# Layers of local attention: output product turned round, probabilities divided before they are transposed, scores and outputs in one group each, and a new order of the parts

## The chip, the cores and the metric

The kernel runs on one NeuronCore of a Trainium2 chip. The metric is the device time of one launch in microseconds. The names of the engines are those of the profile: PE is TensorE (PEld its weight loads), DVE is VectorE, ACT is ScalarE, POOL is GpSimd, SP issues the DMAs.

## What is computed

The reference is a network of eight residual stages on x of 2048 rows by 128 features, all in fp32. Two of the eight are the same stage, `L1_ffn`, with the same weights; the rest (three attention stages, a mixture of experts twice, an attention with a linear kernel) is not touched. Cut to what matters, `L1_ffn` is six times:

```python
# attention with a window: 16 heads of 64, blocks of 32 tokens that look at their own and the block before
qkv = shift_tokens(x) @ Wqkv                       # 128 -> 3 x 1024
q, k = l2norm(q) * q_scale, l2norm(k) * k_scale    # per head of 64
q, k = rotary(q) * scale, rotary(k) / scale
sim = einsum('bhwie,bhwje->bhwij', q, look(k)) * 8 # 32 x 64 per block
attn = softmax(where(mask, -max, sim), -1)
out = einsum('bhwij,bhwje->bhwie', attn, look(v))
x = out @ Wo + x
# feed-forward
xn = layernorm(shift_tokens(x)) * g + b
a, gate = split(xn @ W1 + b1)                      # 2 x 341
x = a * gelu(gate) @ W2 + b2 + x
```

## The kernel before

x is kept transposed (features in partitions, tokens along the free dimension). Each `L1_ffn` is one `Layers` object. It works on tiles of 128 tokens: 6 layers x 2 sequences x 8 tiles = 96 tiles, numbered m. Two `Layers` runs make 192 tiles.

The work of a tile is cut into parts, each a method that issues a few instructions on one engine. `turns` is a software pipeline: turn n goes through the words of `ORDER` once, and a word `name:late` issues that part for tile m = n - late. The feed-forward parts (`BY_BLOCK`) work on four tiles at once and run when m is a multiple of 4, so each of four successive turns holds other feed-forward parts. Inside `manual_schedule` PE, ACT, DVE and POOL execute their instructions in exactly the order in which `turns` issues them; there is no other scheduler. SP's DMAs are not in that list of engines.

```python
for n in range(min(lates), last + max(lates)):
    for stage, args, late, step in order:
        m = n - late
        if 0 <= m < last and m % step == 0:
            stage(m, *args)
```

The parts of one tile in the order of the data, with their lines in the kernel before. The digits after a name in `ORDER` are its arguments: s (0 for q, 1 for k), then u or c, j or r (a half).

- `project` s,u (L1448, PE): one 128x512 half of q or k, into a PSUM bank of the pool `pj` (four banks, shared with v, the outputs, y and the feed-forward).
- `squares` s,u (L1457, ACT) reads that bank into `sq`; `rotate` s,u (L1477, DVE, two instructions) reads the same bank and multiplies it by the rotary tables into `t1` and `t2` (two buffers each).
- `halves` s (L1483, POOL) adds the two halves of `sq`; `lengths` s (L1489, DVE) sums them per head; `inverses` (L1502 to L1504, ACT) makes 1/length.
- `join` s (L1494, POOL) adds `t1` and `t2` into `raw` and so frees the t buffers; `scale` s (L1509, POOL) multiplies by 1/length.
- `flip` s,c (L201 `tqk`, PE): four transposes into a bank of tag `tp` (two banks); `heads` s,c (L1527, ACT) copies them to qT or kT. `carry` (L1542, POOL) hands the last 32 keys to the next tile.
- `project_v` r (L1550, PE), `values` r (L1559, ACT), `windows` r (SP DMAs, `vw_l<-v_l`): v, rearranged so that each block's 64 keys lie in 64 partitions.
- `scores` part 0 and 1 (L1588 the mask in bf16, L1597, PE): products with 64 rows and 32 columns of the array, two banks of tag `big`.
- `below_max` j (L1606, L1607, DVE), `exps` j (L1611, ACT, in place in `pr`, two buffers), `sums` (L1619, L1621, DVE): softmax without the division.
- `flip_p` j (L201 `tpr`, PE) transposes the undivided probabilities, `probabilities` j (L1635, ACT) copies them to `pT`.
- `outputs` part 0 and 1 (L1647, PE): for each block and head a product with `pT` (64 x 32) as the stationary operand and `vw` (64 x 64) as the moving one; tokens come out in partitions, features along the free dimension. Two `pj` banks.
- `divide` r (L1655, DVE) multiplies a bank of outputs by 1/sum into `on`; `flip_o` r (L201 `to`, PE) transposes it back, four transposes each; `features` r (L1672, ACT) copies it to `outT`.
- `project_out` (L1679, PE) makes y, `add_out` (L1693, DVE) adds it to x.
- Feed-forward: `ffn_flip`, `ffn_stats`, `ffn_dev`, `ffn_norm`, `ffn_back`, `ffn_gain` (norm), `gate_in` c and `gate` c (L1753, L1763; Gelu, with a load of the ACT table before it and one back at the end), `value_in` c and `value` c (L1774, L1782), `ffn_out` (L1789), `ffn_add` (L1695).

Of the kernel before, what the change touches and what calls it, by code (L numbers as in the profile page):

```python
# [18 lines left out]
P = 128  # L19
# [11 lines left out]
DEPTH, LH, LD, LW = 6, 16, 64, 32  # L31
# [54 lines left out]
class Net:  # L86
# [288 lines left out]
    def attn_a1(self, key):  # L375
        nc, tc = self.nc, self.tc
        scale = 1.0 / DH**0.5
        with ExitStack() as ctx:
# [166 lines left out]
            def fin(k):  # L545
# [23 lines left out]
    def attn_b1(self, key):  # L569
# [5 lines left out]
        with ExitStack() as ctx:  # L575
# [165 lines left out]
            def xt(k):  # L741
# [309 lines left out]
class Experts:  # L1051
# [223 lines left out]


ORDER = """
    value_in1:11 halves0:-2 join0:-2 add_out:3 flip11:0 divide0:2 divide1:2 project_v0:0 ffn_flip:7
    heads01:0 flip_p0:1 gate_in0:9 heads11:0 value_in0:11 lengths1:-1 value1:11 value_in2:10 values0:0
    scores0:0 lengths0:-2 inverses:-1 project10:-2 ffn_back:8 flip_p1:1 ffn_stats:7 gate0:9 value0:11  # L1280
    ffn_out:11 ffn_dev:7 squares10:-2 sums:1 ffn_norm:7 project11:-2 carry:0 project00:-3 value2:10
    rotate10:-2 scores1:0 probabilities0:1 squares11:-2 project_v1:0 ffn_gain:8 probabilities1:1
    flip_o0:2 scale1:-1 ffn_add:11 gate_in2:9 flip_o1:2 windows0:0 rotate11:-2 squares00:-3 values1:0
    scale0:-1 gate_in1:9 rotate00:-3 features0:2 features1:2 below_max0:0 halves1:-2 gate2:9
    below_max1:0 project01:-3 flip10:-1 gate1:9 squares01:-3 exps0:0 outputs0:1 join1:-2 heads10:-1
    rotate01:-3 project_out:2 flip00:-1 heads00:-1 exps1:0 outputs1:1 flip01:-1 windows1:0
"""
BY_BLOCK = (
    "ffn_flip", "ffn_stats", "ffn_dev", "ffn_norm", "ffn_back", "ffn_gain", "gate_in", "gate",
# [4 lines left out]
class Layers:  # L1294
# [281 lines left out]

    def scores(self, m, part):
        nc, st = self.nc, self.get(m)  # L1580
        key = self.name(m)
        if part == 0:
            st["sc"] = [self.ps.tile([P, 8, 64], F32, tag="big", name=f"sc_{key}_{j}") for j in range(2)]
            first = self.place(m)[2] == 0
            for c in range(4):
                for j in range(2):
                    rows = slice(64 * j, 64 * j + 64)
                    nc.tensor.matmul(  # L1588
                        st["sc"][j][ts(c, 32)].rearrange("p h k -> p (h k)"), self.identb[rows, :],
                        self.wide[rows, 1 if first and c == 0 else 0, :], start=True, stop=False,  # L1590
                    )
        sc = st["sc"]
        for hp in range(4 * part, 4 * part + 4):
            for c in range(4):
                for j in range(2):
                    rows = slice(64 * j, 64 * j + 64)
                    nc.tensor.matmul(  # L1597
                        sc[j][ts(c, 32), hp, :], st["q"][rows, hp, ts(c, 32)],
                        st["k"][rows, hp, ds(32 * c, 64)], start=False, stop=(hp == 7),
                    )  # L1600
# [14 lines left out]
    def sums(self, m):  # L1615
        nc, st, key = self.nc, self.get(m), self.name(m)
        sm = self.small.tile([P, 2, 8], F32, tag="sm", name=f"sm_{key}")
        for j in range(2):
            nc.vector.tensor_reduce(sm[:, j], st["p", j], AX.X, ALU.add)  # L1619
        inv = st["inv"] = self.small.tile([P, 2, 4, 2], F32, tag="inv", name=f"inv_{key}")  # L1620
        nc.vector.reciprocal(inv, sm.rearrange("p j (q r) -> p r q j", r=2))  # L1621

# [11 lines left out]
        pt = st["pT", j] = self.sp.tile([P, 4, P], F32, tag="pT", name=f"pT_{self.name(m)}_{j}", bufs=4)  # L1634
        self.nc.scalar.copy(pt, st["tpr", j])  # L1635

    def outputs(self, m, part):
        nc, st, key = self.nc, self.get(m), self.name(m)
        if part == 0:
            st["av"] = [self.pj.tile([P, 4, 2, LD], F32, tag="pj", name=f"av_{key}_{r}") for r in range(2)]  # L1640
        av = st["av"]
        for q in range(2 * part, 2 * part + 2):
            for j in range(2):
                for c in range(4):
                    for r in range(2):
                        rows = slice(64 * r, 64 * r + 64)
                        nc.tensor.matmul(  # L1647
                            av[r][ts(c, 32), q, j, :], st["pT", j][rows, q, ts(c, 32)],
                            st["vw"][rows, c, ts(2 * q + j, LD)], start=True, stop=True,
                        )  # L1650

    def divide(self, m, r):
        st = self.get(m)
        on = st["on", r] = self.sp.tile([P, 4, 2, LD], F32, tag="on", name=f"on_{self.name(m)}_{r}")
        self.nc.vector.tensor_tensor(  # L1655
            on, st["av"][r], st["inv"][:, r, :, :, None].to_broadcast([P, 4, 2, LD]), ALU.mult
        )

    def flip_o(self, m, r):
        st = self.get(m)
        st["to", r] = self.net.to_psum(
            self.ps, "tp", lambda q: st["on", r][:, q].rearrange("p j d -> p (j d)"),
            f"to_{self.name(m)}_{r}",
        )

    def features(self, m, r):
        st = self.get(m)
        if r == 0:  # L1670
            st["o"] = self.qp.tile([P, 8, P], F32, tag="outT", name=f"outT_{self.name(m)}")
        self.nc.scalar.copy(st["o"].rearrange("p (q r) t -> p r q t", r=2)[:, r], st["to", r])  # L1672

    def project_out(self, m):
        i, b, a = self.place(m)
# [293 lines left out]
```

## Time and profile before

| | |
|---|---|
| time, median of 3 runs | 3995.49 us (3991.46 to 3996.87) |
| span of the profiled execution | 3987.0 us (its total is not given on the page) |
| first and last `y_l` group (L1679) | starts at 637.1 and 3957.2 us |
| busy PE / DVE / ACT / POOL | 96% / 78% / 61% / 64% of the span |
| mean granted clock of PE | 0.970 of full speed |
| busy in 606 to 2217 and 2387 to 3987 us, inside the two Layers runs (3211 us) | PE 3182.8, DVE 2555.2, ACT 2073.7, POOL 2173.4 us |
| DMA over the span | 281 MB, mean 71 GB/s |

How to read it. A line of a group gives the source line, the engine, the operation, out<-in by tile names, the shapes, the count; then after the bar the busy time, the mean duration of one in ns; then the idle time of that engine just before these instructions and what ended it. Busy PE is modelled from pipelined matmuls: neighbouring groups overlap in the list, so the cost of a group is best taken from its start to the start of the next one. One fp32 matmul is two records. In the chain of waits each piece is what the end of the run was waiting for at that time.

### The profile page before, as it was taken

The page shows a single profiled execution, that of the slowest core. Times are in us where ns is not written, and L with a number is a line of the kernel's source. Part 1 is how long each engine was busy: PE and PEld are TensorE (multiplying, and loading weights), DVE is VectorE, ACT ScalarE, POOL GpSimd, SP SyncE. Part 2 cuts the span into 40 slices and gives each one's busy share as a digit, 9 for nine tenths or more (in the row PEclk, how much of TensorE's full clock was granted, in tenths as well). Part 3 has the DMA queues.
Part 4 walks back from the last instruction along what each step waited for, and adds up shares of the span by engine and source line. Part 5 has one row for each costly group of instructions (what it writes and reads, how often), then busy time and mean ns, then how long its engine had stood idle before and what let it go on. Part 6 is the DMA issues. An engine that isn't in the chain of part 4 may idle for free.

```text
span 3987.0 us, 156275 instructions
## 1 busy us (share of the span) xinstructions
PE 3825.6 (96%) x67372; PEld 2521.5 (63%) x67372; DVE 3116.1 (78%) x6012; ACT 2414.0 (61%) x4582; POOL 2535.5 (64%) x1638
## 2 busy tenths in 40 slices
PE   7898979999999999999999779999999999999998
PEld 5646436666666666666666446666666666666665
DVE  7775877778787878787887667887878787878786
ACT  3444437766666666666666458666666666666665
POOL 4541448776766667767675467766767767666662
PEclk8899979999999999999999779999999999999999
DMA  3030313232333333323222033333333323332222
GB/s 87 2 85 8 79 62 75 67 92 69 78 84 75 78 78 73 88 72 77 63 70 67 9 95 70 75 85 75 86 71 73 92 68 77 85 76 67 66 68 54
DMA packets 217397, 281.11 MB, mean 71 GB/s; under 512 B 52493, under 2 KB 108682, under 8 KB 216586
## 3 DMA queue, kind: packets, MB, share of 16 engines
q1 hardware_dynamic: 216714, 271.12, 27.9%
q8 instruction: 536, 8.78, 1.0%
q14 instruction: 147, 1.20, 0.1%
HBM read 69.46 MB, written 3.28 MB: 18 GB/s over the span
## 4 chain that ended last, share of the span: by engine, by line
PE 87%; DVE 6%; DMA 2%; POOL 2%; ACT 1%; issue 1%; SPq 0%; DVEq 0%; POOLq 0%; ACTq 0%
PE pj_l L1448 17%; PE y_l L1679 9%; PE pv_l L1550 9%; PE tqk_l L201 9%; PE av_l L1647 8%; PE sc_l L1597 7%; PE tpr_l L201 4%; PE to_l L201 4%; PE fg_l L1753 3%; PE fy_l L1789 3%; PE fa_l L1774 3%; PE sc_l L1588 2%; DMA f0share_e<-f0d_e 1%; PE f0S_e L1239 1%; DVE t_l L1477 1%
## 5 line engine op out<-in xcount | busy, mean ns | idle before, releaser
L1477 DVE TENSOR_TENSOR t_l<-pj_l,rot_l 128x512 f32<-128x512 f32 x1536 | 968.1, 684 | 368.6 <-ACT sq_l L1457 356.6
L1494 POOL TENSOR_TENSOR raw_l<-t_l,t_l 128x1024 f32<-128x1024 f32 x384 | 907.8, 2364 | 532.5 <-DVE on_l L1655 285.0
L1448 PE MATMUL pj_l<-wqkv_l,x_l 128*128 128x512 f32 x1536 | 785.9, 614 | 6.5 <-DVE t_l L1477 4.2
L1509 POOL TENSOR_TENSOR raw_l<-raw_l,rn_l 128x1024 f32<-128x1024 f32 x384 | 723.2, 1902 | 94.6 <-ACT rn_l L1504 87.4
L1483 POOL TENSOR_TENSOR sq_l<-sq_l 128x512 f32<-128x512 f32 x384 | 490.8, 1278 | 311.8 <-ACT sq_l L1457 308.7
L1457 ACT ACTIVATE sq_l<-pj_l 128x512 f32<-128x512 f32 x768 | 461.5, 603 | 369.6 <-PE pj_l L1448 367.6
L201 PE MATMUL tqk_l<-ident_sb,raw_l 128*128 128x128 f32 x3072 | 452.7, 278 | 15.5 <-POOL raw_l L1509 13.9
L1527 ACT COPY qT_l<-tqk_l 128x512 f32<-128x512 f32 x384 | 224.8, 585 | 387.9 <-PE tqk_l L201 387.8
L201 PEld LDWEIGHTS tqk_l<-ident_sb,raw_l 128*128 128x128 f32 x3072 | 356.4, 142 | 160.7 <-issue 121.3
L1550 PE MATMUL pv_l<-wqkv_l,x_l 128*128 128x512 f32 x768 | 416.4, 624 | 6.1 <-DVE ln_xn_fl L1733 5.3
L1679 PE MATMUL y_l<-outT_l,wo_l 128*128 128x128 f32 x3072 | 393.7, 281 | 0.0
L1597 PEld LDWEIGHTS sc_l<-kT_l,qT_l 64*32 64x32 f32 x24576 | 295.4, 105 | 155.5 <-issue 145.1
L1679 PEld LDWEIGHTS y_l<-outT_l,wo_l 128*128 128x128 f32 x3072 | 357.5, 191 | 18.3 <-issue 1.0
L1448 PEld LDWEIGHTS pj_l<-wqkv_l,x_l 128*128 128x128 f32 x1536 | 256.3, 192 | 172.1 <-issue 111.2
L1647 PE MATMUL av_l<-vw_l,pT_l 64*32 64x64 f32 x24576 | 360.5, 224 | 2.1 <-issue 1.7
L1559 ACT COPY v_l<-pv_l 128x512 f32<-128x512 f32 x384 | 225.1, 586 | 225.4 <-PE pv_l L1550 205.5
L1655 DVE TENSOR_TENSOR on_l<-av_l,inv_l 128x512 f32<-128x512 f32 x384 | 247.4, 686 | 121.5 <-PE av_l L1647 121.3
L1647 PEld LDWEIGHTS av_l<-vw_l,pT_l 64*32 64x32 f32 x24576 | 294.2, 105 | 70.0 <-issue 63.6
L1597 PE MATMUL sc_l<-kT_l,qT_l 64*32 64x64 f32 x24576 | 329.8, 223 | 0.3 <-issue 0.3
L201 PEld LDWEIGHTS tpr_l<-ident_sb,pr_l 128*128 128x128 f32 x1536 | 189.1, 141 | 152.3 <-issue 116.8
L1607 DVE TENSOR_TENSOR pr_l<-sc_l,mx_l 128x512 f32<-128x512 f32 x384 | 265.6, 692 | 13.2
L201 PEld LDWEIGHTS to_l<-ident_sb,on_l 128*128 128x128 f32 x1536 | 183.2, 141 | 128.4 <-issue 110.9
(317 smaller groups left out, 6208.9 us busy)
## 6 DMA issues: line engine op xcount, KB each, us to landing
vw_l<-v_l SPq DMA_DIRECT2D x3024, 64.0 KB
wqkv_l<-in_Wqkv SPq DMA_DIRECT2D x36, 512.0 KB
f0share_e<-f0d_e SPq DMA_DIRECT2D x64, 256.0 KB
rot_l<-in_rotary SPq DMA_DIRECT2D x24, 512.0 KB
wo_l<-in_Wo SPq DMA_DIRECT2D x12, 512.0 KB
w_l<-in_W SPq DMA_DIRECT2D x12, 341.0 KB
a0rows<-a0both SPq DMA_DIRECT2D x4, 512.0 KB
a0qk<-a0rows SPq DMA_DIRECT2D x32, 64.0 KB
```

Of the source, the lines that this page charges most:

```text
L201: self.nc.tensor.transpose(tp[:, c, :], src(c), self.ident)
L1448: self.nc.tensor.matmul(pj.rearrange("p h d -> p (h d)"), self.x[b][0][:, ts(a, P)], self.w[i]["qkv"][:, ds(INNER * s + 512 * u, 512)], st ...
L1457: self.nc.scalar.activation(st["sq", s][:, u], st["pj", s, u], AF.Square)
L1477: self.nc.vector.tensor_tensor(to, st["pj", s, u], tabs[:, k, None, ts(w, LD // 2)].to_broadcast(half), ALU.mult)
L1483: self.nc.gpsimd.tensor_tensor(sq[:, 0], sq[:, 0], sq[:, 1], ALU.add)
L1494: self.nc.gpsimd.tensor_tensor(r.rearrange("p h u d -> p u h d"), st["t1", s], st["t2", s], ALU.add)
L1509: self.nc.gpsimd.tensor_tensor(r, r, st["rn"][:, ts(s, LH), None].to_broadcast([P, LH, LD]), ALU.mult)
L1550: self.nc.tensor.matmul(pj, self.x[b][0][:, ts(a, P)], self.w[i]["qkv"][:, ds(2 * INNER + 512 * r, 512)], start=True, stop=True,)
L1597: nc.tensor.matmul(sc[j][ts(c, 32), hp, :], st["q"][rows, hp, ts(c, 32)], st["k"][rows, hp, ds(32 * c, 64)], start=False, stop=(hp == 7),)
L1607: nc.vector.tensor_tensor(p, st["sc"][j], mx[:, :, None].to_broadcast([P, 8, 64]), ALU.subtract)
L1647: nc.tensor.matmul(av[r][ts(c, 32), q, j, :], st["pT", j][rows, q, ts(c, 32)], st["vw"][rows, c, ts(2 * q + j, LD)], start=True, stop=True,)
L1679: self.nc.tensor.matmul(y[:, 0:P], self.w[i]["o"][:, c, :], st["o"][:, c, :], start=(c == 0), stop=(c == 7))
```

## The change

Scores and outputs are issued in one group each instead of two parts. The outputs are formed by features: `vw` (64 x 64) is now the stationary operand and `pT` (64 x 32) the moving one, so features come out in partitions and `features` copies the banks straight to `outT`. `flip_o` goes, and the tile `on` with it. The division moves from the outputs to the probabilities: `divide` j multiplies `pr` by 1/sum in place after `sums` and before `flip_p`. `ORDER` is written anew, with the earliest part at -4 instead of -3, outputs at 2 instead of 1, and other positions for nearly all parts.

```diff
 ORDER = """
-    value_in1:11 halves0:-2 join0:-2 add_out:3 flip11:0 divide0:2 divide1:2 project_v0:0 ffn_flip:7
-    heads01:0 flip_p0:1 gate_in0:9 heads11:0 value_in0:11 lengths1:-1 value1:11 value_in2:10 values0:0
-    scores0:0 lengths0:-2 inverses:-1 project10:-2 ffn_back:8 flip_p1:1 ffn_stats:7 gate0:9 value0:11
-    ffn_out:11 ffn_dev:7 squares10:-2 sums:1 ffn_norm:7 project11:-2 carry:0 project00:-3 value2:10
-    rotate10:-2 scores1:0 probabilities0:1 squares11:-2 project_v1:0 ffn_gain:8 probabilities1:1
-    flip_o0:2 scale1:-1 ffn_add:11 gate_in2:9 flip_o1:2 windows0:0 rotate11:-2 squares00:-3 values1:0
-    scale0:-1 gate_in1:9 rotate00:-3 features0:2 features1:2 below_max0:0 halves1:-2 gate2:9
-    below_max1:0 project01:-3 flip10:-1 gate1:9 squares01:-3 exps0:0 outputs0:1 join1:-2 heads10:-1
-    rotate01:-3 project_out:2 flip00:-1 heads00:-1 exps1:0 outputs1:1 flip01:-1 windows1:0
+    add_out:3 gate2:10 values0:0 exps1:0 exps0:0 scale1:-1 lengths1:-2 flip00:-1 flip01:-1 outputs:2
+    heads00:-1 heads01:-1 sums:0 value_in2:11 flip10:-1 values1:0 halves0:-3 project10:-3
+    features0:2 flip11:-1 value_in0:10 lengths0:-3 features1:2 divide0:0 ffn_back:8 heads10:-1
+    value2:11 join1:-2 project11:-3 rotate10:-3 heads11:-1 divide1:0 project00:-4 squares10:-3
+    squares11:-3 halves1:-3 value0:10 gate_in0:9 inverses:-2 ffn_gain:8 ffn_flip:7 gate_in1:9
+    value_in1:10 scores:-1 ffn_out:11 rotate11:-3 ffn_stats:7 join0:-3 rotate00:-4 scale0:-2
+    ffn_dev:7 project01:-4 gate0:9 windows0:0 squares00:-4 gate1:9 flip_p0:0 flip_p1:0 squares01:-4
+    gate_in2:9 ffn_norm:7 probabilities0:0 value1:10 ffn_add:11 probabilities1:0 project_v0:-1
+    rotate01:-4 carry:-1 below_max0:-1 project_out:2 windows1:0 below_max1:-1 project_v1:-1
 """
...
-    def scores(self, m, part):
+    def scores(self, m):
...
-        for hp in range(4 * part, 4 * part + 4):
+        for hp in range(8):
...
-        inv = st["inv"] = self.small.tile([P, 2, 4, 2], F32, tag="inv", name=f"inv_{key}")
-        nc.vector.reciprocal(inv, sm.rearrange("p j (q r) -> p r q j", r=2))
+        inv = st["inv"] = self.small.tile([P, 2, 8], F32, tag="inv", name=f"inv_{key}")
+        nc.vector.reciprocal(inv, sm)
+
+    def divide(self, m, j):
+        p = self.get(m)["p", j]
+        self.nc.vector.tensor_tensor(
+            p, p, self.get(m)["inv"][:, j, :, None].to_broadcast([P, 8, 64]), ALU.mult
+        )
...
-    def outputs(self, m, part):
+    def outputs(self, m):
...
-            st["av"] = [self.pj.tile([P, 4, 2, LD], F32, tag="pj", name=f"av_{key}_{r}") for r in range(2)]
-        for q in range(2 * part, 2 * part + 2):
-            for j in range(2):
-                for c in range(4):
+        av = st["av"] = [self.pj.tile([P, 4, P], F32, tag="pj", name=f"av_{key}_{r}") for r in range(2)]
+        for q in range(4):
+            for c in range(4):
+                for j in range(2):
                     for r in range(2):
                         rows = slice(64 * r, 64 * r + 64)
                         nc.tensor.matmul(
-                            av[r][ts(c, 32), q, j, :], st["pT", j][rows, q, ts(c, 32)],
-                            st["vw"][rows, c, ts(2 * q + j, LD)], start=True, stop=True,
+                            av[r][ts(j, LD), q, ts(c, 32)], st["vw"][rows, c, ts(2 * q + j, LD)],
+                            st["pT", j][rows, q, ts(c, 32)], start=True, stop=True,
                         )
-    def divide(self, m, r):
-        st = self.get(m)
-        on = st["on", r] = self.sp.tile([P, 4, 2, LD], F32, tag="on", name=f"on_{self.name(m)}_{r}")
-        self.nc.vector.tensor_tensor(
-            on, st["av"][r], st["inv"][:, r, :, :, None].to_broadcast([P, 4, 2, LD]), ALU.mult
-        )
-    def flip_o(self, m, r):
...
-        self.nc.scalar.copy(st["o"].rearrange("p (q r) t -> p r q t", r=2)[:, r], st["to", r])
+        self.nc.scalar.copy(st["o"].rearrange("p (q r) t -> p r q t", r=2)[:, r], st["av"][r])
```

More of the change, by code (lines that the diff above doesn't have):

```diff
@@ L1574, in windows @@
                 nc.sync.dma_start(to, self.get(m - 1)["v"][96:128, r, :])
-    def scores(self, m, part):
+    def scores(self, m):
         nc, st = self.nc, self.get(m)
         key = self.name(m)
-        if part == 0:
-            st["sc"] = [self.ps.tile([P, 8, 64], F32, tag="big", name=f"sc_{key}_{j}") for j in range(2)]
-            first = self.place(m)[2] == 0
-            for c in range(4):
-                for j in range(2):
[L1587 to L1590, printed above, removed]
-                    )
-        sc = st["sc"]
-        for hp in range(4 * part, 4 * part + 4):
+        sc = st["sc"] = [self.ps.tile([P, 8, 64], F32, tag="big", name=f"sc_{key}_{j}") for j in range(2)]
+        first = self.place(m)[2] == 0
+        for c in range(4):
+            for j in range(2):
+                rows = slice(64 * j, 64 * j + 64)
+                nc.tensor.matmul(
+                    sc[j][ts(c, 32)].rearrange("p h k -> p (h k)"), self.identb[rows, :],
+                    self.wide[rows, 1 if first and c == 0 else 0, :], start=True, stop=False,
+                )
+        for hp in range(8):
             for c in range(4):
@@ L1619, in sums @@
             nc.vector.tensor_reduce(sm[:, j], st["p", j], AX.X, ALU.add)
-        inv = st["inv"] = self.small.tile([P, 2, 4, 2], F32, tag="inv", name=f"inv_{key}")
-        nc.vector.reciprocal(inv, sm.rearrange("p j (q r) -> p r q j", r=2))
+        inv = st["inv"] = self.small.tile([P, 2, 8], F32, tag="inv", name=f"inv_{key}")
[4 more added lines that the diff above has]
+            p, p, self.get(m)["inv"][:, j, :, None].to_broadcast([P, 8, 64]), ALU.mult
+        )
     def flip_p(self, m, j):
@@ L1635, in probabilities @@
         self.nc.scalar.copy(pt, st["tpr", j])
-    def outputs(self, m, part):
+    def outputs(self, m):
         nc, st, key = self.nc, self.get(m), self.name(m)
-        if part == 0:
-            st["av"] = [self.pj.tile([P, 4, 2, LD], F32, tag="pj", name=f"av_{key}_{r}") for r in range(2)]
-        av = st["av"]
-        for q in range(2 * part, 2 * part + 2):
-            for j in range(2):
-                for c in range(4):
+        av = st["av"] = [self.pj.tile([P, 4, P], F32, tag="pj", name=f"av_{key}_{r}") for r in range(2)]
+        for q in range(4):
+            for c in range(4):
+                for j in range(2):
                     for r in range(2):
@@ L1647, in outputs @@
                         nc.tensor.matmul(
-                            av[r][ts(c, 32), q, j, :], st["pT", j][rows, q, ts(c, 32)],
-                            st["vw"][rows, c, ts(2 * q + j, LD)], start=True, stop=True,
-                        )
-    def divide(self, m, r):
-        st = self.get(m)
-        on = st["on", r] = self.sp.tile([P, 4, 2, LD], F32, tag="on", name=f"on_{self.name(m)}_{r}")
-        self.nc.vector.tensor_tensor(
-            on, st["av"][r], st["inv"][:, r, :, :, None].to_broadcast([P, 4, 2, LD]), ALU.mult
-        )
-    def flip_o(self, m, r):
[L1662 to L1666, printed above, removed]
+                            av[r][ts(j, LD), q, ts(c, 32)], st["vw"][rows, c, ts(2 * q + j, LD)],
+                            st["pT", j][rows, q, ts(c, 32)], start=True, stop=True,
+                        )
     def features(self, m, r):
```

## The prediction

> **What bounds the kernel now.** I read the page first (shares, slices, chain), then the chain in order of time inside one Layers turn, then the groups with their idle time, then the timelines. The page:
>
> ```profile
> PE 3825.6 (96%) x67372; PEld 2521.5 (63%) x67372; DVE 3116.1 (78%) x6012; ACT 2414.0 (61%) x4582; POOL 2535.5 (64%) x1638
> PEclk8899979999999999999999779999999999999999
> PE 87%; DVE 6%; DMA 2%; POOL 2%; ACT 1%; issue 1%; SPq 0%; DVEq 0%; POOLq 0%; ACTq 0%
> ```
>
> TensorE is busy nearly throughout, at full clock in both Layers runs (slices 6 to 21 and 24 to 39), and it is 87% of the chain. The chain in order of time, one turn:
>
> ```profile
> 2007.90 0.79 PE sc_l L1597 x53
> ...
> 2009.74 0.87 PE to_l L201 x8
> ...
> 2011.92 0.94 PE av_l L1647 x56
> 2012.86 1.98 PE y_l L1679 x16
> ...
> 2015.28 0.79 PE av_l L1647 x53
> ...
> 2019.25 0.34 PE sc_l L1588 x8
> 2019.59 0.66 PE sc_l L1597 x49
> ```
>
> It passes from TensorE group to TensorE group; no other engine is on it. In the window from 1000 to 2000 us the two adds of L1693 occur 120 times and the reciprocal of L1621 59 times: some 59.5 turns, 16.8 us each. The others wait inside the turn:
>
> ```profile
> L1477 DVE TENSOR_TENSOR t_l<-pj_l,rot_l 128x512 f32<-128x512 f32 x1536 | 968.1, 684 | 368.6 <-ACT sq_l L1457 356.6
> L1494 POOL TENSOR_TENSOR raw_l<-t_l,t_l 128x1024 f32<-128x1024 f32 x384 | 907.8, 2364 | 532.5 <-DVE on_l L1655 285.0
> L1483 POOL TENSOR_TENSOR sq_l<-sq_l 128x512 f32<-128x512 f32 x384 | 490.8, 1278 | 311.8 <-ACT sq_l L1457 308.7
> ```
>
> The first line matters most. `rotate` (L1477) needs only the PSUM bank that `project` filled, yet it waits for `squares` (L1457): two readers of one bank are put one behind the other, in the order in which the program names them.
>
> The page gives no total of the profiled execution; its span is 3987.0, 8.5 below the median of 3995.49 (runs 3991.46 to 3996.87), so 8.5 us lie around it, and I add differences to the median. A measurement of this kernel can tell 0.2%, 8 us, from no change.
>
> **The change on TensorE.** Removed: eight transposes per tile (to_l), 0.87 us of the chain; their copy only changes its source. Scores in one group: each entry into the small-tile mode costs 0.10 (fg before scores runs 0.96 from start to next start, pj before another full-array group 0.86) and each group has its own fill and end; between 0.1 and 0.5 saved, 0.35 taken. Outputs in one group save one entry too, 0.1, but change shape: instead of loads of 32 columns with 64 moving, in eight array parts, loads of 64 columns with 32 moving, in four. Moving work per part is halved and loading doubled. Rows:
>
> ```profile
> L1647 PEld LDWEIGHTS av_l<-vw_l,pT_l x24576: 102/106/108, 621.6 to 3951.9; 64*32 64x32 f32 x200
> L951 PEld LDWEIGHTS a0s<-a0qk x1024: 127/132/227, 24.9 to 156.9; 8*64 8x64 f32 x171
> 202.26 0.95 PE L1129 MATMUL f0lg_e<-f_sb,f0x_e 128*128 128x8 f32 x8
> ```
>
> L1129 moves 8 columns per load of 128 and makes 8 steps from 202.26 to 203.07, some 0.11 each: it is bound by loading, 0.87 ns per column. 64 columns are then 56 ns; 128 loads in four parts are 1.8 us, with fill and end 2.0, against 0.94 + 0.79 = 1.73. Bounds: 1.3 if only issue counts (today's groups without their second fill), 3.6 if the two column parts share a path (2 x 128 x 56 / 4). I take 2.0, nearest to L1129. Sum: -0.87 - 0.35 - 0.1 + 0.27 = -1.05 us per turn. TensorE alone would need 15.75 us.
>
> **The change on the other engines.** `divide` keeps its count and size (two of 128x512, 686 ns), but now stands between `sums` and the transposes of p, and reads two SBUF operands. `features` keeps two copies. `windows` keeps its DMAs on SP; outputs come two turns after instead of one, and av_l's wait for DMA is 1.5 us in the whole run today, so this costs nothing; without that distance a transfer would show before outputs. av and y keep two and one of the four pj banks; av is released by ScalarE rather than VectorE.
>
> The new order is what decides. In the built lists `rotate10` now precedes `squares10`, and `rotate00` precedes `squares00` (both squares wait for VectorE; the second halves still go squares first, and `rotate01` waits for ScalarE). And `rotate00` takes the t buffer (two exist) that `join0` frees, so it waits for `join0`, which stands on GpSimd behind `halves1`, which needs `squares11`. Behind `rotate01` on VectorE are queued `below_max0/1`, which `exps` of the next turn wait for, and behind these `sums`, `divide0`, `rotate10`. That is a closed ring, once per turn. Steps by starts in the timelines, among them:
>
> ```profile
> 2010.63 0.68 DVE L1606 TENSOR_REDUCE mx_l<-sc_l 128x8 f32<-128x512 f32 x1
> 2011.34 0.69 DVE L1607 TENSOR_TENSOR pr_l<-sc_l,mx_l 128x512 f32<-128x512 f32 x1
> 2011.95 0.68 DVE L1606 TENSOR_REDUCE mx_l<-sc_l 128x8 f32<-128x512 f32 x1
> 2009.37 2.37 POOL L1494 TENSOR_TENSOR raw_l<-t_l,t_l 128x1024 f32<-128x1024 f32 x1
> ```
>
> - ScalarE: two exps, 0.52 + 0.63 = 1.15
> - VectorE: sums with reciprocal 1.47, lengths0 0.59, divide0 0.61, rotate10 1.29: 3.96
> - ScalarE: squares10, squares11: 0.49 + 0.60 = 1.09
> - GpSimd: halves1 1.23 (2008.14 to 2009.37), join0 2.37: 3.60
> - VectorE: rotate00 1.29; ScalarE: squares00, squares01 1.09
> - VectorE: rotate01 1.22, below_max twice 0.71 + 0.61 + 0.71 + 0.69: 3.94
>
> Together 16.1, and with seven hand-overs (square ends 2006.01, rotate starts 2006.04; some 0.05 on average, more to GpSimd) 16.45 us in a turn without FFN work. FFN steps on the ring per four turns: value2 0.64, gate1 between the two squares 0.63, ffn_norm and ffn_add 2.8 of which 1.1 lie beside squares: 3.0, so 0.74 per turn. That gives 17.2, and 0.1 for places where TensorE is late as well: 17.3. The ring ends later than TensorE's 15.75, so the TensorE gain is lost, and the turn grows by 0.5. What waits next is TensorE itself: at `flip10` for the tp bank that `heads00` (queued behind the exps) has to empty, and at matmuls that need a pj bank from `squares`.
>
> Some 184 of 192 turns are full: +92 us. Filling: the earliest part now is 4 turns ahead instead of 3, and the filling turns, 14.9 to 15.0 us today by the starts of the first y_l groups, also go at the ring's 16.4: one turn and five times 1.4, 22 us per run, 44 for two. 3995.5 + 92 + 44 = 4131, said as 4130. On the ring divide0 costs 0.6 per turn; it falls into a time when GpSimd is through `join1` and waits for `squares11`.
>
> Bounds on divide: VectorE with two SBUF operands, beside GpSimd's adds in the expert stage, shows
>
> ```profile
> L1236 DVE SCALAR_TENSOR_TENSOR f0xe_e<-f0share_e,f0x_e x64: 676/692/1759, 205.3 to 491.0; 128x512 f32<-128x512 f32 x64
> ```
>
> so 0.68 to 1.76 us; I take 0.69 because of that gap on GpSimd. The Trainium skill (SBUF — State Buffer, "Who interferes with whom") speaks against the change here: a VectorE instruction with two SBUF inputs and a GpSimd instruction that reads SBUF exclude each other, and the later one stands still until the first is through. By that rule, with the divides falling anywhere, GpSimd's rows (two each of 1.28, 2.36 and 1.90 in 16.8 us) make an average wait of (1.28² + 2.36² + 1.90²) / 16.8 = 0.65 per divide, 120 us over 184 turns and a time near 4250; by the gap it costs nothing.
>
> **Rivals.**
>
> *TensorE stays the bound (0.13).* Place: the ring above. It decides from the point where the ring, with its FFN share, is under 15.8 us: if a bank's second reader need not wait, rotate10, squares and rotate00 overlap, some 1.3 + 1.1 come off, and 17.2 falls to 14.8. Then the time is 3995 - 192 x 1.05 = 3794, with the longer filling 3820; with the ring half closed, up to 3960. For it: TensorE fills 87% of the chain today and loses work. Against it: the 356.6 us of L1477.
>
> *Weight loading is dearer (0.06).* At 3.6 for outputs TensorE needs 17.35, and against the ring some 17.7: +165 + 44, about 4205. Against it: the loads of av_l on eight parts overlap well today (64 in 0.79).
>
> *The divides meet GpSimd (0.10).* One divide on the ring at up to 1.76 adds up to 1.07, 0.6 on average: 0.6 x 184 = 110, about 4240.
>
> That the ring is closed and the time ends near 4130 I give 0.68; the remaining 0.03 is no change, a ring of 16.7 with a filling that overlaps the norms before it. So faster 0.13, same 0.03, slower 0.84. The range takes the ring without its FFN share and a short filling (16.75 a turn, about 4000) up to the divides' case, 4240; outside are the fast rival and the tail of the slow ones, 0.2.
>
> **What would show it.** Right: TensorE busy below 93% in the Layers slices with the clock still full; no to_l; av_l starts 2.0 us before the next group; ScalarE sq_l idle because of VectorE t_l; VectorE t_l idle because of GpSimd raw_l; the chain's VectorE, ScalarE and GpSimd shares up by tens of per cent. Wrong: the chain still over 80% TensorE, or L1457 with no VectorE releaser; av_l near 3.6; divides (pr_l<-pr_l,inv_l) far above 0.7.

## The result, and the profile after

The changed kernel takes 4227.8 us (median of 4 runs, 4223.8 to 4232.1) against 3995.6 us: a ratio of 1.0589, 95% interval 1.0574 to 1.0604. It is 232 us slower; the forecast was 4130, 134 slower, with a range up to 4240. The profiled execution of after took 4232.1 us, of which 4230.4 are its span; the spans of the two profiles differ by 243.4 us.

The page of after, the lines that answer to the first block of the prediction:

```profile
PE 3828.3 (90%) x65836; PEld 2555.4 (60%) x65836; DVE 3150.2 (74%) x6012; ACT 2352.3 (56%) x4586; POOL 2507.6 (59%) x1638
PEclk7898978999999999999999669999999999999999
DVE 16%; PE 10%; ACT 4%; SPq 3%; POOL 3%; issue 2%; DMA 2%; ACTq 0%; DVEq 0%; POOLq 0%
```

TensorE has 1536 fewer matmul records (the transposes of to_l are gone) and still the same busy time, in a longer span. The chain could be followed back over some 40% of the span only; in that part VectorE leads, where TensorE had 87% before. The groups (after the bar: busy us, mean ns; then the idle time ahead and what ended most of it):

```profile
L1477 DVE TENSOR_TENSOR t_l<-pj_l,rot_l 128x512 f32<-128x512 f32 x1536 | 989.5, 686 | 718.2 <-POOL raw_l L1494 392.6
L1483 POOL TENSOR_TENSOR sq_l<-sq_l 128x512 f32<-128x512 f32 x384 | 489.3, 1274 | 1174.3 <-ACT sq_l L1457 850.9
L1494 POOL TENSOR_TENSOR raw_l<-t_l,t_l 128x1024 f32<-128x1024 f32 x384 | 906.3, 2360 | 0.0
L1457 ACT ACTIVATE sq_l<-pj_l 128x512 f32<-128x512 f32 x768 | 424.7, 595 | 679.4 <-DVE t_l L1477 640.3
L1623 DVE TENSOR_TENSOR pr_l<-pr_l,inv_l 128x512 f32<-128x512 f32 x384 | 265.3, 692 | 0.2
```

`rotate` (L1477) now waits for GpSimd's join (raw_l, L1494), `squares` (L1457) for `rotate`, `halves` (L1483) for `squares`: three engines stand behind one another. The durations of the instructions themselves are those of before; only the waits grew. One turn in order of time, from the timelines of VectorE, ScalarE and GpSimd of after (start, length, engine and line; in brackets the idle time ahead and its releaser):

```profile
1070.93 1.29 DVE L1477 TENSOR_TENSOR t_l<-pj_l,rot_l 128x512 f32<-128x512 f32 x2 [2.42 <-POOL raw_l L1494]
1072.33 1.08 ACT L1457 ACTIVATE sq_l<-pj_l 128x512 f32<-128x512 f32 x2 [3.66 <-DVE t_l L1477]
1073.45 1.29 DVE L1477 TENSOR_TENSOR t_l<-pj_l,rot_l 128x512 f32<-128x512 f32 x2 [1.23 <-ACT sq_l L1457]
...
1077.56 1.15 ACT L1609 ACTIVATE pr_l<-pr_l 128x512 f32<-128x512 f32 x2 [2.68 <-DVE pr_l L1605]
...
1080.77 0.68 DVE L1623 TENSOR_TENSOR pr_l<-pr_l,inv_l 128x512 f32<-128x512 f32 x1
1081.74 1.29 DVE L1477 TENSOR_TENSOR t_l<-pj_l,rot_l 128x512 f32<-128x512 f32 x2 [0.29 <-PE pj_l L1448]
1083.12 1.31 ACT L1457 ACTIVATE sq_l<-pj_l 128x512 f32<-128x512 f32 x2
1084.51 1.27 POOL L1483 TENSOR_TENSOR sq_l<-sq_l 128x512 f32<-128x512 f32 x1 [4.87 <-ACT sq_l L1457]
1085.74 2.36 POOL L1494 TENSOR_TENSOR raw_l<-t_l,t_l 128x1024 f32<-128x1024 f32 x1
1088.13 1.29 DVE L1477 TENSOR_TENSOR t_l<-pj_l,rot_l 128x512 f32<-128x512 f32 x2 [2.38 <-POOL raw_l L1494]
```

This is the ring of the prediction, link by link: rotate00, squares00, rotate01 with below_max, exps, sums with divide0, rotate10, squares10 and 11, halves1, join0, and rotate00 again 17.20 us later.

Where the 243.4 us are, by the starts of the first and last instructions of pj_l and y_l in the two Layers runs (us from the start of the span):

| | before | after | difference |
|---|---|---|---|
| ahead of the first pj_l (stages that are not touched) | 562.8 | 572.4 | +9.5 |
| filling: first pj_l to first y_l, both runs | 74.2 + 76.1 | 107.6 + 104.8 | +62.1 |
| first to last y_l, both runs | 1569.2 + 1570.4 | 1651.7 + 1645.3 | +157.4 |
| last y_l of run 1 to first pj_l of run 2 (with an untouched stage) | 104.5 | 120.9 | +16.4 |
| behind the last y_l | 29.7 | 27.7 | -2.0 |

In the 80 middle turns of the first run a turn takes 17.74 us; before it took 16.86.

What the prediction did not have is TensorE's clock. In after it is at half speed for 71.7 and 68.3 us between the first and the last y_l of the two runs; before for 0 and 3.4. One such place, by windows of after (TensorE's granted clock is the third number from the end), and TensorE's timeline of it:

```profile
1073.00:1076.40 3.40, 3.40 (x103) 2.49 (x103) 2.85 (x5) 1.88 (x4) 3.26 (x5) 1.00 0.55 174
1076.40:1079.80 3.40, 1.23 (x56) 1.15 (x49) 3.25 (x7) 2.24 (x5) 3.24 (x2) 1.00 0.21 51
1079.80:1083.20 3.40, 3.40 (x10) 1.74 (x9) 3.08 (x7) 2.48 (x6) 0.00 (x0) 0.51 0.47 110
1083.20:1086.60 3.40, 3.40 (x29) 1.39 (x35) 1.72 (x3) 3.19 (x7) 2.09 (x2) 0.99 0.43 99
```

```profile
1075.03 2.12 PE L1649 MATMUL av_l<-pT_l,vw_l 64*64 64x32 f32 x128
1079.33 0.63 PE L201 MATMUL tqk_l<-ident_sb,raw_l 128*128 128x128 f32 x4 [2.17 <-ACT qT_l L1527]
1079.79 1.84 PE L1448 MATMUL pj_l<-wqkv_l,x_l 128*128 128x512 f32 x2
```

TensorE waits 2.17 us for the tp bank that `heads00` empties behind the exps; the next 3.4 us are granted at 0.51, and pj_l takes 1.84 us where 1.1 is usual. On the ring that shows as the 0.29 us that rotate10 waits for pj_l and as squares of 1.31 us.

### The profile page after: what moved, and what is told of

The parts are those of the page before. It is cut to its first block, busy times and chain, and to the rows that moved or that the text cites. A ratio compares the mean times of both kernels' runs of the same rounds, so it can differ in the third digit from the quotient of the medians.

```text
span 4230.4 us, 153519 instructions
## 1 busy us (share of the span) xinstructions
PE 3828.3 (90%) x65836; PEld 2555.4 (60%) x65836; DVE 3150.2 (74%) x6012; ACT 2352.3 (56%) x4586; POOL 2507.6 (59%) x1638
## 3 DMA queue, kind: packets, MB, share of 16 engines
q1 hardware_dynamic: 216714, 271.12, 26.2%
## 5 line engine op out<-in xcount | busy, mean ns | idle before, releaser
L1477 DVE TENSOR_TENSOR t_l<-pj_l,rot_l 128x512 f32<-128x512 f32 x1536 | 989.5, 686 | 718.2 <-POOL raw_l L1494 392.6
L1483 POOL TENSOR_TENSOR sq_l<-sq_l 128x512 f32<-128x512 f32 x384 | 489.3, 1274 | 1174.3 <-ACT sq_l L1457 850.9
L1494 POOL TENSOR_TENSOR raw_l<-t_l,t_l 128x1024 f32<-128x1024 f32 x384 | 906.3, 2360 | 0.0
L1448 PE MATMUL pj_l<-wqkv_l,x_l 128*128 128x512 f32 x1536 | 834.7, 647 | 15.4 <-ACT sq_l L1457 7.9
L1457 ACT ACTIVATE sq_l<-pj_l 128x512 f32<-128x512 f32 x768 | 424.7, 595 | 679.4 <-DVE t_l L1477 640.3
L201 PEld LDWEIGHTS tqk_l<-ident_sb,raw_l 128*128 128x128 f32 x3072 | 379.2, 148 | 448.9 <-issue 276.3
L1609 ACT ACTIVATE pr_l<-pr_l 128x512 f32<-128x512 f32 x384 | 220.8, 622 | 484.9 <-DVE pr_l L1605 484.9
L1649 PE MATMUL av_l<-pT_l,vw_l 64*64 64x32 f32 x24576 | 451.7, 221 | 36.2 <-issue 34.0
L1649 PEld LDWEIGHTS av_l<-pT_l,vw_l 64*64 64x64 f32 x24576 | 425.0, 134 | 74.7 <-issue 62.9
L1665 PE MATMUL y_l<-outT_l,wo_l 128*128 128x128 f32 x3072 | 380.7, 277 | 17.0 <-ACT sq_l L1457 16.4
L1604 DVE TENSOR_REDUCE mx_l<-sc_l 128x8 f32<-128x512 f32 x384 | 261.6, 681 | 10.6 <-PE sc_l L1595 10.6
L1527 ACT COPY kT_l<-tqk_l 128x512 f32<-128x512 f32 x384 | 223.3, 615 | 77.4 <-PE tqk_l L201 76.9
L1623 DVE TENSOR_TENSOR pr_l<-pr_l,inv_l 128x512 f32<-128x512 f32 x384 | 265.3, 692 | 0.2
L1489 DVE TENSOR_REDUCE ss_l<-sq_l 128x16 f32<-128x512 f32 x384 | 252.4, 658 | 11.3 <-POOL sq_l L1483 5.7
```

The costliest lines, as they stand in the source:

```text
L201: self.nc.tensor.transpose(tp[:, c, :], src(c), self.ident)
L1448: self.nc.tensor.matmul(pj.rearrange("p h d -> p (h d)"), self.x[b][0][:, ts(a, P)], self.w[i]["qkv"][:, ds(INNER * s + 512 * u, 512)], st ...
L1457: self.nc.scalar.activation(st["sq", s][:, u], st["pj", s, u], AF.Square)
L1477: self.nc.vector.tensor_tensor(to, st["pj", s, u], tabs[:, k, None, ts(w, LD // 2)].to_broadcast(half), ALU.mult)
L1483: self.nc.gpsimd.tensor_tensor(sq[:, 0], sq[:, 0], sq[:, 1], ALU.add)
L1494: self.nc.gpsimd.tensor_tensor(r.rearrange("p h u d -> p u h d"), st["t1", s], st["t2", s], ALU.add)
```

## The experiments

All times below are medians of four or more executions, each set beside the kernel before (3995.7 to 3997.3 us in these sets). "Theory R" is the closed ring.

**Opening the ring.** Three kernels change one or both of the two links that close it.

```diff
 # swap: in ORDER
-project11:-3 rotate10:-3 heads11:-1 divide1:0 project00:-4 squares10:-3 squares11:-3
+project11:-3 squares10:-3 rotate10:-3 heads11:-1 divide1:0 project00:-4 squares11:-3
...
-join0:-3 rotate00:-4 scale0:-2 ffn_dev:7 project01:-4 gate0:9 windows0:0 squares00:-4
+join0:-3 squares00:-4 rotate00:-4 scale0:-2 ffn_dev:7 project01:-4 gate0:9 windows0:0
```

> The changed kernel with squares10 put before rotate10 and squares00 before rotate00 in the list of parts; nothing else. Theory R (the turn is a closed ring: exps, sums and rotate10 on VectorE, squares, halves1 and join0 on GpSimd, rotate00, rotate01, below_max, exps): the squares no longer wait for rotate10, the ring loses some 1 us of its 17.35 us per turn, so about 4228 - 184 x 1 = 4045 (4000 to 4100), and the idle time of ScalarE sq_l behind VectorE t_l falls to a small part of 640 us. Rival T (TensorE with the dearer output product, 2.15 instead of 1.74 us, sets the turn): 4228 within 20, since TensorE has the same work. Rival S (the swap only moves the wait: VectorE now stands behind ScalarE): no gain or a loss, 4220 to 4280, with t_l idle behind sq_l grown by as much as sq_l behind t_l shrank.

```diff
 # t3: in rotate
-st[n, s] = self.qp.tile([P, 2, LH, LD // 2], F32, tag=n, name=f"{n}_{self.name(m)}_{s}")
+st[n, s] = self.qp.tile([P, 2, LH, LD // 2], F32, tag=n, name=f"{n}_{self.name(m)}_{s}", bufs=3)
```

> The changed kernel with three buffers instead of two for t1 and t2; the order of the parts is that of the changed kernel. Theory R: rotate00 no longer waits for join0 of the tile before, the ring is open at that place, and TensorE sets the turn again at some 15.7 us: 4228 - 184 x 1.65 = 3925 (3880 to 3990), below the kernel before; idle time of VectorE t_l behind GpSimd raw_l goes from 392.6 us to under 100. Rival T (TensorE sets the turn): 4228 within 20. Rival S (the two readers of one bank are enough to close the ring without the t buffers): 4100 to 4200, sq_l behind t_l still above 500 us.

With both edits (`swap_t3`):

> The changed kernel with both edits: squares10 and squares00 ahead of rotate10 and rotate00, and three buffers for t1 and t2. Theory R: one opening is enough, so the same as with three buffers alone, within 30 us (3880 to 3990). Rival S (each edit opens only its part): clearly below each of the two alone. Rival T: 4228 within 20.

Measured: swap 4094.0 (ratio to before 1.0241, 1.0222 to 1.0260), three t buffers 4048.5 (1.0125, 1.0099 to 1.0150), both 4030.6 (1.0089, 1.0070 to 1.0107). So swap gives 134 us back, three buffers 179, both 197. The waits of swap, from its groups:

```profile
L1477 DVE TENSOR_TENSOR t_l<-pj_l,rot_l 128x512 f32<-128x512 f32 x1536 | 979.1, 684 | 498.1 <-ACT sq_l L1457 262.1 <-POOL raw_l L1494 230.3 <-ACT fh_l L1749 2.3
L1457 ACT ACTIVATE sq_l<-pj_l 128x512 f32<-128x512 f32 x768 | 461.3, 604 | 411.3 <-PE pj_l L1448 394.2 <-DVE ss_l L1489 11.3 <-issue 4.2
```

`squares` no longer waits for `rotate` (640.3 us in after), and `rotate` does not wait longer for `squares` (262.1 us, 278.5 in after), so rival S of that run fell too. Three of the waits of after, and then, with three t buffers, what is left of them (us in total, times, longest):

```profile
ACT sq_l L1457 <- DVE t_l L1477: 640.3, 336, 5.1
DVE t_l L1477 <- POOL raw_l L1494: 392.6, 193, 2.7
PE tqk_l L201 <- ACT qT_l L1527: 143.9, 89, 5.3
```

```profile
ACT sq_l L1457 <- DVE t_l L1477: 272.4, 284, 3.8
PE tqk_l L201 <- ACT qT_l L1527: 42.3, 30, 3.9
```

The shares of its chain, from its page:

```profile
PE 65%; DVE 19%; ACT 5%; issue 4%; POOL 3%; DMA 3%; SPq 1%; DVEq 0%; ACTq 0%; POOLq 0%
```

The wait for raw_l, 193 times in after, is no longer among the waits that the view lists, and TensorE leads the chain again. That rules out rival T. Both edits together are 18 us faster than three buffers alone, at the edge of the noise: the two intervals overlap slightly. But theory R's 3925 was not reached: opened, the turn is 16.95 us, not 15.7. Part of this is that the 15.7 was too low: TensorE alone needs some 16.3 (below). And between the first and the last y_l TensorE is at half clock for 85 us with three t buffers, and stops inside the outputs for 61. The divides change as well: their mean went from 692 ns in after to 837 with three t buffers and 948 with both edits. VectorE's and GpSimd's timelines with three t buffers:

```profile
1070.06 2.17 DVE L1623 TENSOR_TENSOR pr_l<-pr_l,inv_l 128x512 f32<-128x512 f32 x1
1069.32 2.36 POOL L1494 TENSOR_TENSOR raw_l<-t_l,t_l 128x1024 f32<-128x1024 f32 x1
```

GpSimd's addition ends at 1071.68, the divide 0.55 later. Of the 384 divides of that run 66 start inside a GpSimd addition or product; on average 1.05 us of that instruction is then left, and they take 1.60. The others take 0.68. That this costs time here is not shown: with both edits the divides are longer still and the time is shorter.

**The control.**

```diff
 # before_t3: in rotate of the kernel before
-st[n, s] = self.qp.tile([P, 2, LH, LD // 2], F32, tag=n, name=f"{n}_{self.name(m)}_{s}")
+st[n, s] = self.qp.tile([P, 2, LH, LD // 2], F32, tag=n, name=f"{n}_{self.name(m)}_{s}", bufs=3)
```

> The kernel before with three buffers for t1 and t2; control. Theory R: TensorE sets its turn, the ring is not closed there, so no change: 3995 within 10. Rival S (the two t buffers hold up any order of these parts): faster by 1% or more.

Measured: 3994.2, ratio 0.9998 (0.9982 to 1.0014). The t buffers are no limit in the order of before.

**A link taken out.** Without the divides (the probabilities stay undivided):

```diff
 # no_divide: in ORDER
-features1:2 divide0:0 ffn_back:8
+features1:2 ffn_back:8
-heads11:-1 divide1:0 project00:-4
+heads11:-1 project00:-4
```

> The changed kernel without its two divide instructions per tile (the probabilities stay undivided; all else, the order too, as in the changed kernel). Theory R (closed ring): divide0 stands on the ring, between sums and rotate10, so 0.61 us per turn come off, 184 x 0.61 = 112 us, 4228 - 112 = 4116 (4090 to 4150). Rival T (TensorE with its dearer output product sets the turn): 4228 within 20, since TensorE keeps all its work. Rival D (VectorE's load as a whole sets the turn, not the ring): both divides, 1.36 us, come off, 4228 - 250 = 3978 or below.

Measured: 4146.7 (1.0378, 1.0351 to 1.0406), 81 us less than after. A middle turn went from 17.74 to 17.16, by 0.58; divide0 alone is 0.61. TensorE's clock was lower for a shorter time in this run (92 us between the first and the last y_l, 140 in after), but that is not where the gain comes from: turns with no feed-forward part on the ring, in which TensorE was neither at half clock nor stopped, went from 16.78 to 16.21, by 0.57. So VectorE's load as a whole (1.36 us per turn) is not the limit, and TensorE's work is not either: only the divide on the ring counted. Not all of the expected 112 us came, since over all turns from the first to the last y_l the profiles differ by 95 us, 0.50 per turn, and the filling did not shrink (212.4 us in after, 214.5 here).

**TensorE's stops.** With three t buffers:

```diff
 # t3_split: three t buffers, and in ORDER (the method takes a part again)
-outputs:2 heads00:-1 heads01:-1 sums:0 value_in2:11 flip10:-1 values1:0
+outputs0:2 heads00:-1 heads01:-1 sums:0 value_in2:11 flip10:-1 outputs1:2 values1:0
```

> The changed kernel with three t buffers (4048.5 us) and the output product in two parts again, the second behind flip10, nothing else. In the run with three t buffers TensorE stops inside the output group, mostly between its 100th and 126th record, for 1.3 to 2.7 us, 37 times in the run, 61 us in all, without a releaser. Theory G (the long group of short instructions is what makes it stop): stops inside the outputs under 15 us, time 4048 - 50 = 4000 (3975 to 4020). Rival N (the stops come after a certain number of instructions wherever that falls): the same 50 to 60 us, in other groups, time 4048 within 15. A longer group costs no entry: a second entry costs 0.1 per turn, +18 us, in either case included.

Measured: 4094.5 (1.0245, 1.0228 to 1.0262), 46 us slower than in one group, so theory G's time fell. The stops inside the outputs went from 61 to 37 us only, and ScalarE's wait for the outputs (outT_l behind av_l) grew from 110.6 to 294.7 us, with the copies of the next parts queued behind it. One place between two halves is not enough to remove the stops. What cost the 46 us, the second entry or the later end of the outputs, this run does not separate.

**The groups alone, in the kernel before.**

```diff
 # before_scores: in ORDER of before
-values0:0 scores0:0 lengths0:-2
+values0:0 lengths0:-2
-rotate10:-2 scores1:0
+rotate10:-2 scores0:0 scores1:0
```

> The kernel before with its two parts of scores issued one behind the other, at the place of the second; nothing else. The prediction put 0.35 us per tile (0.1 to 0.5) on this: 3996 - 192 x 0.35 = 3929 (3900 to 3977). Rival M (the starts in the trace of after are right: a group of both parts takes 1.54 to 1.60 us behind the mask's 0.23, as the two parts did): no gain, 3996 within 10. Rival F (a long run of short instructions outpaces the fetch of instructions, 16 KB a packet, and makes TensorE stop): stops of over 1 us inside sc_l appear and the time is 3996 to 4040.

```diff
 # before_outputs: in ORDER of before
-exps0:0 outputs0:1 join1:-2
+exps0:0 join1:-2
-exps1:0 outputs1:1
+exps1:0 outputs0:1 outputs1:1
```

> The kernel before with its two parts of outputs issued one behind the other, at the place of the second; nothing else. The prediction put 0.1 us per tile on the entry saved: 3996 - 19 = 3977. Rival M (the entry costs nothing that shows): 3996 within 10. Rival F (fetch of instructions): stops of over 1 us inside av_l appear, as in the changed kernel, where 27 of them took 42 us; the time is 4000 to 4050, the half-speed clock after a stop included.

Measured: scores 3969.5 (0.9933, 0.9915 to 0.9950), 27.7 us or 0.14 per tile; outputs 3963.5 (0.9918, 0.9893 to 0.9943), 33.7 us or 0.18 per tile. Rival M fell in both: a group fewer does save, though the starts inside sc_l show nothing of it, because part of the saving is in the group ahead, which no longer runs out before the change of tile size (y_l goes from 1.89 to 1.79 in before_outputs). The outputs in one group of old shape take 1.51 us (median, start to next start) instead of 2 x 0.79. The stops of rival F came in before_outputs, whose waits of TensorE show the line below, but not its time of 4000 to 4050; in before_scores none of over 1 us came inside the scores:

```profile
PE av_l L1647 <- issue: 22.8, 23, 1.9
```

"issue" is a wait with no releaser in the profile. The profile of before has 1.7 us of it there, in four waits (6.6 us of "issue" before TensorE's matmuls in all).

**The new product in other orders.** Four orders of my own, with the new product and the divided probabilities. own_a, with two t buffers:

```diff
+    exps0:1 windows0:1 rotate01:-2 windows1:1 heads00:0 add_out:3 exps1:1 flip01:0 value_in0:11
+    features0:2 flip11:0 value_in1:11 features1:2 join1:-1 heads01:0 heads11:0 sums:1 lengths1:-1
+    value0:11 halves0:-2 project_v0:0 join0:-2 project10:-2 values0:0 value_in2:10 ffn_flip:7 divide1:1
+    value1:11 gate_in0:9 squares10:-2 project11:-2 ffn_out:11 divide0:1 inverses:-1 rotate10:-2
+    ffn_stats:7 scores0:0 ffn_back:8 flip_p1:1 gate0:9 ffn_gain:8 value2:10 squares11:-2 flip_p0:1
+    lengths0:-2 ffn_dev:7 ffn_norm:7 probabilities1:1 scale1:-1 gate_in2:9 project00:-3 gate2:9
+    scale0:-1 rotate11:-2 carry:0 project_v1:0 halves1:-2 scores1:0 ffn_add:11 squares00:-3 values1:0
+    probabilities0:1 rotate00:-3 gate_in1:9 flip10:-1 gate1:9 below_max0:0 project01:-3 project_out:2
+    squares01:-3 flip00:-1 outputs0:1 outputs1:1 below_max1:0 heads10:-1
```

> The new output product and the division ahead of the transposes, with two t buffers, but another order of the parts: earliest part at -3 as in the kernel before, squares ahead of rotate in three of four banks, scores in two parts, divides early in the next turn. Theory R (the order alone cost the time; the new product leaves TensorE some 16.2 us per turn against 16.86): 3995 - 184 x 0.65 = 3875, 3860 to 3960 with some stops. Rival P (the new product itself makes TensorE stop, whatever the order): 3995 or more.

(In fact squares stand ahead of rotate in all four banks.) own_b has three t buffers, scores in one group, outputs in two:

```diff
+    squares10:-2 windows0:0 scores0:0 halves0:-2 scores1:0 project11:-2 value1:11 scale1:-1 value2:10
...
+    outputs0:1 rotate01:-3 flip01:-1 flip11:-1 exps1:0 outputs1:1 join0:-2 windows1:0 heads11:-1
...
```

> As the run own_a, with three t buffers and yet another order made in the same way. Theory R: 3860 to 3960 as well, within 30 us of own_a, since no ring is closed in either. Rival S (two t buffers hold up any order with this product): clearly faster than own_a, by 50 us or more. Rival P: 3995 or more.

Measured: own_a 3934.4 (ratio 0.9841, 0.9822 to 0.9859), own_b 3955.6 (0.9904, 0.9882 to 0.9927). Both are faster than the kernel before, own_a by 62 us and than the changed kernel by 293. So the new product is not what costs; rival P fell, and the order alone turned a gain into a loss. The page of own_a:

```profile
PE 3724.8 (95%) x65836; PEld 2486.0 (63%) x65836; DVE 3376.6 (86%) x6012; ACT 2421.4 (62%) x4582; POOL 2524.2 (64%) x1638
PE 76%; DVE 4%; ACT 2%; issue 2%; POOL 1%; DMA 0%; SPq 0%; POOLq 0%; ACTq 0%; DVEq 0%
```

TensorE is the bound again: a middle turn is 16.37 us against 16.86 before, the filling is 72.9 and 74.6 us as before, and 27 us lie at half clock between the y_l. VectorE's 86%, against 78% before, come from divides that meet GpSimd (mean 1373 ns, the longest tenth over 2.7 us); they do not set the time, since VectorE has 4% of the chain.

Then the stops again, with all four small groups apart (own_c, own_d):

```diff
 # own_c
+    features1:2 add_out:3 project_v0:0 heads01:0 value0:11 ffn_back:8 value1:11 ffn_flip:7 heads11:0
...
+    ffn_gain:8 ffn_out:11 gate_in0:9 rotate10:-2 ffn_norm:7 scores0:0 windows0:0 inverses:-1
+    probabilities0:1 squares10:-2 join0:-2 gate0:9 project11:-2 project_v1:0 flip_p1:1 values1:0
+    ffn_add:11 probabilities1:1 scores1:0 rotate11:-2 project00:-3 lengths0:-2 gate_in2:9 scale1:-1
...
+    project01:-3 outputs0:1 heads10:-1 below_max0:0 gate1:9 exps1:0 squares01:-3
```

> The new output product in an order of my own as in own_a, but with scores and outputs in two parts each and at least 1.7 us of other TensorE work between any two of these four groups, and with the divides where GpSimd is between its additions. Theory F (stops come from long runs of short instructions): stops inside av_l and sc_l, 30 us in own_a, fall under 10 us, little half clock in the steady turns, 3934 - 30 = 3900 (3870 to 3925). Rival N (stops come at the same rate wherever the groups are): 3934 within 20, 25 us or more of stops. The divides' mean, 1373 ns in own_a, should be near 690 in either case.

own_d:

```diff
+    lengths0:-2 heads11:0 scale1:-1 value1:11 add_out:3 squares10:-2 gate_in2:9 project11:-2 value2:10
+    join0:-2 ffn_out:11 ffn_stats:7 gate_in0:9 rotate10:-2 ffn_dev:7 value_in0:10 flip_p0:1 scores0:0
+    scale0:-1 gate2:9 ffn_norm:7 project00:-3 flip_p1:1 squares11:-2 rotate11:-2 project_v1:0 gate0:9
+    probabilities0:1 squares00:-3 value0:10 ffn_add:11 gate_in1:9 scores1:0 probabilities1:1 rotate00:-3
...
+    below_max0:0 gate1:9 outputs0:1 join1:-2 squares01:-3 below_max1:0 heads10:-1 project_v0:-1
+    flip01:-1 rotate01:-3 heads00:-1 flip11:-1 exps0:0 outputs1:1 exps1:0 heads01:-1 value_in1:10
...
```

> Made as own_c, with another order that keeps the same two conditions. Theory F: within 25 us of own_c, stops under 10 us. Rival N: as for own_c. If own_c and own_d differ by more than 40 us, neither theory holds all that counts, and the waits decide.

Measured: own_c 3980.6 (0.9953, 0.9934 to 0.9972), own_d 3995.8 (0.9988, 0.9969 to 1.0006). Theory F was right on the stops, which fell from 30 us in own_a to 1.3 and 2.7, and the divides' mean is 779 and 694 ns; and it was wrong on the time. A further group on its own costs, as before_scores and before_outputs had shown with the other sign: a middle turn of own_c is 16.54, with 2.32 in av_l (2.27 in own_a, stops included), 3.74 instead of 3.53 in pj_l and 1.88 instead of 1.78 in y_l, the groups ahead of an entry. So in these orders the stops cost less than what avoiding them took. That the entries are all of this price is not shown, for own_c and own_d are whole new orders: of the 42 us between the profiles of own_a and own_c, 13 are in the filling.

own_a with scores in one group as well was not run.

## Why the prediction was right, and where it was not

**The bound.** Right. That the order, not TensorE, would set the turn, by a ring through join0 and the t buffers, is shown by the three kernels that open it and by the control; that divide0 is a link, by its removal. Of the signs named in advance the waits came, sq_l behind t_l and t_l behind raw_l, and to_l is gone. Two did not: TensorE is busy for 93.6% of 680 to 2331 us, not below 93%, at a granted clock of 0.98, not full; and the group after av_l starts 3.27 us after av_l's start (median), not 2.0, since TensorE waits there. That 4228 lies inside the range owes something to luck: the upper end, 4240, was set for divides that meet GpSimd on the ring, and they did not; the loss was 232 us where 134 was forecast.

**The size of the ring.** Too small: the term of +0.5 us per turn (92 us) measured +0.88 in the middle turns and +157 from first to last y_l. The prediction added 16.45 us for a turn without feed-forward work, 0.74 for that work and 0.1 "for places where TensorE is late as well". The trace of after tells the three apart, if its 156 middle turns (both runs, from one rotate00 to the next) are sorted by whether TensorE was at half clock or stopped inside scores or outputs in them; 113 were free of both.

| us per turn | foreseen | measured |
|---|---|---|
| undisturbed, no feed-forward part on the ring (one turn in four) | 16.45 | 16.78 |
| feed-forward share (the four kinds of undisturbed turn average 17.48) | 0.74 | 0.70 |
| TensorE late (all 156 turns average 17.72) | 0.1 | 0.24 |

So most of the missing 0.4 is in the ring itself, at full clock: the instructions have the sizes of the prediction, but the hand-overs between them make some 0.66 and not 0.35. The rest is TensorE's lateness, which was added with the clock taken as full. The turn shown above is of the first kind with half clock in it: 17.20 instead of 16.78, by rotate10's wait for pj_l (0.29) and slower squares10 and 11 (0.17). That half clock and stops lengthen the turns is read from turns with and without them in one trace; no run takes the half clock away by itself.

**The filling.** 44 foreseen, 62.1 measured. own_a, whose earliest part is at -3 and which has no ring, fills in the time of before. With three t buffers it is still 96.0 and 96.1 us, so the larger part, 42 of 62, goes with the order and not with the ring. Whether the earlier start alone makes it is not shown: own_c and own_d start at -3 too and fill in 160.4 and 173.7 us for both runs, own_a in 147.5. At half clock are 60.3 and 54.1 us of after's filling, against 26.5 and 26.2.

**TensorE's own sum.** The -1.05 us was too good. to_l is right (0.873 us per middle turn before, none after). Scores in one group: -0.14, not -0.35, just inside the bounds. Outputs in one group: -0.18 rather than -0.1. The turned product: like for like, 1.51 to 2.15 us, +0.64; the prediction compared 2.0 with 1.73. Sum: -0.87 - 0.14 - 0.18 + 0.64 = -0.55, so TensorE alone needs some 16.3 and not 15.75, an estimate from these runs. Own_a bears it out roughly: with scores still split and 0.16 of stops the sum gives 16.6, and its turn is 16.37. So the fast rival's 3794, which needs 15.8, was out of reach by these figures even with the ring open; 3934 is the best that a run showed.

**The divides.** The value 0.69 by the gap on GpSimd was right (692 ns), and the rival's 4240 fell in this kernel. But the gap is the ring's own work: GpSimd is idle there because halves1 waits. With the ring open and nothing else moved, the divides do meet GpSimd (66 of 384). The Trainium skill ("SBUF — State Buffer", "Who interferes with whom") has the rule: the later of the two stands still until the first is through. The runs agree and put a number on it: the rest of GpSimd's instruction plus 0.55 us, a little less than the 0.68 of a divide alone.

**Untouched stages.** Not foreseen: 9.5 us ahead of the first Layers run, and 16.4 between the two, where the stage runs at a granted clock of 0.52 instead of 0.67 (windows of before, then of after):

```profile
2226.00:2302.00 76.00, 57.86 (x168) 29.03 (x168) 52.80 (x165) 32.20 (x88) 43.45 (x39) 0.67 0.02 6
```

```profile
2349.00:2443.00 94.00, 75.89 (x168) 37.38 (x168) 53.82 (x164) 32.35 (x88) 42.65 (x39) 0.52 0.02 5
```

All ten profiles of kernels with the new product have 97 to 104 us of half clock between the last y_l of run 1 and the first pj_l of run 2, all four with the old one 56 to 72. Why the clock of this stage differs with the kernel ahead of it stays open. The 9.5 us ahead are no effect of the change: with the same instructions there, that stretch was 563 to 574 us over these 14 profiles, and the profile of before has the shortest. So the spans differ by 243 us and the medians by 232. For the same reason the prediction read 8.5 us "around" the span: it set the span of one execution against the median of others. In the runs with both numbers some 2 us lie around it.

**The lower end of the range.** It is called the ring without its feed-forward share at 16.75 a turn; by the prediction's own sum it would be 16.45.

## What to carry to other kernels

When a change frees the bounding engine, first look at the order that comes with it: follow every wait for a buffer and every bank with two readers round one turn, and if the walk comes back to its start, its length is the turn when it exceeds the work of the freed engine. Opening one link (here a third buffer) shows within one run whether such a ring is there, and an order made for the new work gave 1.6% where the ring had lost 5.9%. A gap into which new work seems to fit for nothing may be the ring's own idle time, and goes when the ring is opened.

## What the runs showed of the hardware

**The clock falls after short stops.** In the first Layers run of after there are 19 stretches at half clock between 670 and 2150 us; their starts lie on one grid of 3.41 us, and in the window ahead of each TensorE was idle for 1.3 to 3.0 us. Between the first and the last y_l of all 14 profiles other windows of this grid with up to 2.03 us idle stayed at full speed, and none with more did. A wait of TensorE of 2 us can so cost another 1.7 us of its work, an estimate: half of 3.41. The Trainium skill ("TensorE: Matmul & The Clock Gate", "HAM oscillation — how this bites in real kernels") gives the rule "no PE-idle gaps >~3.4µs"; here gaps of 1.3 to 2.17 us were enough in 18 of the 19 cases.

**TensorE stops when it seems to have run out of instructions.** A stop inside the outputs of after, by TensorE's timeline:

```profile
932.20 2.18 PE L1649 MATMUL av_l<-pT_l,vw_l 64*64 64x32 f32 x107
936.30 0.72 PE L1649 MATMUL av_l<-pT_l,vw_l 64*64 64x32 f32 x21 [1.92 <-issue]
```

The list of DMA queues has one for instructions (packets, MB, share):

```profile
q8 instruction: 525, 8.60, 0.9%
```

That is 16 KB a packet. The stops of over 1 us inside the outputs in four runs (after, three t buffers, own_a, before_outputs) are 85; 84 of them end 1.13 to 1.61 us after a packet of this queue has landed, while packets come some 6 to 7 us apart. That fits a group of 128 short matmul records with their 128 loads that outpaces the fetch now and then, 24 times by over 1 us in the 192 tiles of after, with the new product as with the old; no run changes the fetch itself. In parts of 64, well apart (own_c, own_d), TensorE hardly stops. Parts of 64 alone do not do it: in own_b, whose two output parts have only eight transposes between them, 13 stops of over 1 us remain.

**Two readers of one bank.** `squares` and `rotate` read the same bank in the order in which the program names them; to name the reader first that the longer chain waits for was worth 134 us in the changed kernel, and nothing had to be moved but two words.
